# Graph attention over 128 feature rows: a product on another engine, row maxima placed by transfers, one table written later

## The chip, the core and the metric

The kernel runs on one core of a Trainium2 chip. The metric is the device time of one execution in microseconds (us); the time of a kernel is the median of several executions. The engines are TensorE (PE; its weight loads are shown apart as PEld), VectorE (DVE), ScalarE (ACT), GpSimd (POOL) and SyncE (SP), which here only issues transfers.

## The reference

The inputs are node features x (3327 x 128), a weighted adjacency matrix adj (3327 x 3327, mostly zero) and five weight matrices. Two layers follow one another, both with a residual:

```python
h = relu(layernorm(x))
x = x + relu((D^-1/2 (adj + I) D^-1/2 h) @ W0)          # layer 0
h = relu(layernorm(x))
q, k, v = ((h @ W.T).reshape(128, 3327, 8) for W in (Wq, Wk, Wv))
a = einsum('dnh,dmh->dnm', q, k) * 128**-0.5 + adj + adj  # 128 x 3327 x 3327
a = softmax(a, axis=2)
x = x + einsum('dnm,dmh->dnh', a, v).reshape(3327, 1024) @ Wo.T   # layer 1
```

Layer 1 is 128 independent attentions ("heads" below, index d), each of 3327 queries and 3327 keys with a depth of only 8, and adj is added twice to every score.

## The kernel before, in words

Layer 0 and the tables for layer 1 take the first tenth of the time. `find_edges` lists the nonzero entries of every row of adj (at most 135, 27, 20, 15 or 13 slots a row, by tile of 128 rows). Since nearly all of adj is zero, the attention is computed without adj, and the edges are added apart.

**Tables by node.** `by_nodes` (L461) turns k, v and q from one row per head into one row per node, by transposes on TensorE, copies on ScalarE (L489) and VectorE (L490) and a store: `kn_d`, `vn_d`, `qn_d`, in this order, 26 tiles of 128 nodes each.

**Edges ahead.** `over_edges` (L495) then treats the last three tiles of queries, tile by tile: for each slot a gather of 128 rows of `kn_d`, a product with q (L520), a sum over the 8 depths (L521), the bias (L525); then the maximum (L532), the exponential, a gather of `vn_d`, a product (L548) and sums on TensorE (L556). A planner of the framework orders this part. The other 23 tiles' edges go on GpSimd beside the attention (`edges_beside`): its instructions are a list with estimated times, from which `edges_on` takes some at each key tile, so that they last for a little over five sixths of the heads.

**Attention.** Queries are cut into seven chunks, in the order 383, 384, then five of 512. For every chunk there are 128 heads, so 896 heads in all; with 26 key tiles each. This part is written in its final order by hand. While head g gets its weights and output, the row maxima of heads g+1 and g+2 are computed beside it:

- `weight(t)`, for key tile t: a matmul gives 128 keys x 512 queries (`pt`, L865), ScalarE takes the exponential (`e`, L873). The operands are held in two halves of 64 partitions, and matmuls of the two halves stand beside one another.
- `products`: e times v, summed in PSUM (`po`, L892), six tiles later.
- `part` and `left`: matmuls (`ps`, L791) give scores by query, and VectorE takes their maxima (`top`, L776 and L810). `left` treats the two odd key tiles at the end of a row group. When a row is done, L818 writes `neg`, the negated maximum per query.
- `halve` (L822): GpSimd splits `neg` into two float32r numbers, `halves` (128 x 4 x 2).
- `place` (L827): four transposes (three in narrow chunks) bring the halves into two rows, `pt_max`; one tile later `below_q` copies them to two rows below q (L838, ScalarE) and from there to the second half of partitions (L839, GpSimd). The key operand has ones in these rows, so `pt` comes out less its row maximum.
- At the end of a head `evacuate` copies `po`, `fold_up` transposes it (`pt_out`), `divide` adds the four groups (L943) and the edges' part (L945, GpSimd), and `by_sums` takes the reciprocal (L954) and the product with it (`o`, L955), both on VectorE, and stores `o` to DRAM from SP (L960).

The later steps are put off by a counter of key tiles: `later(n, step)` runs a step n tiles on. `evacuate` runs in the next head at tile 5, `fold_up` five later, `divide` one later, `by_sums` eight later, at about tile 20. `attend_beside` puts the maxima's steps on tiles: the last row group of head g+1 on tiles 0 to 5 of head g, `halve` at tile 7, and `place` at

```python
behind.setdefault(t + 3, []).append(of_next[1])
behind.setdefault(min(t + 3 + PLACED, MJ - 2), []).append(of_next[2])
```

which, with PLACED = 8, is tile 15. The loads of a head's q, k, v and edges (`load`, L726) are issued by SP three heads ahead, at the start of head g for head g+3, into four buffers in turn: up to three transfers for the edges (L739), eight for q (L751), four for k (L753) and two for v (L754). SP issues in program order and waits where a transfer must wait.

Of the kernel before, what the change touches and what calls it, by code (L numbers as in the profile page):

```python
# [2 lines left out]

# [6 lines left out]
F32 = mybir.dt.float32  # L10
F32R = mybir.dt.float32r
# [22 lines left out]
U = 4  # L34
LATE = 6
FOLDED = 5
PLACED = 8
GATHERED = 27


# [43 lines left out]
def kernel(  # L84
# [376 lines left out]
    def by_nodes():  # L461

        nc.scalar.activation(factor, edge_adj, AF.Exp, scale=-2.0)
        nc.vector.tensor_scalar(factor, factor, -1.0, 1.0, ALU.mult, ALU.add)
        nc.vector.tensor_scalar(bias, edge_adj, 0.0, NO_EDGE, ALU.is_le, ALU.mult)
        nc.vector.tensor_tensor(bias, bias, edge_adj, ALU.add)
        with (
            tc.tile_pool(name="by_head", bufs=2) as by_head,
            tc.tile_pool(name="by_node", bufs=6) as by_node,
            tc.tile_pool(name="ps_turn", bufs=4, space=PSUM) as ps_turn,  # L470
        ):
            for src, dst, more in ((k_d, kn_d, 0), (v_d, vn_d, P), (q_d, qn_d, 0)):
                for n0 in range(0, N, W):
                    w = min(W, N - n0)
                    xs = by_head.tile([P, w * H], F32, tag=f"xs{w}", name="xs")
                    nc.sync.dma_start(out=xs, in_=src[:D, n0 * H : (n0 + w) * H])
                    xs = xs.rearrange("d (n h) -> d h n", h=H)
                    for i in range((w + P - 1) // P):
                        r = min(P, w - i * P)
                        ps = ps_turn.tile([P, H, P], F32, tag="ps", name="ps_turn")  # L480
                        for h in range(H):
                            nc.tensor.transpose(
                                ps[:r, h, :], xs[:, h, i * P : i * P + r], ident
                            )
                        row = by_node.tile([P, E + more], F32, tag=f"row{more}", name="row")
                        if more:
                            nc.gpsimd.memset(row[:, E:], 1.0)
                        to = row[:r, :E].rearrange("p (h d) -> p h d", h=H)
                        nc.scalar.copy(to[:, : H // 2], ps[:r, : H // 2])  # L489
                        nc.vector.tensor_copy(to[:, H // 2 :], ps[:r, H // 2 :])  # L490
                        nc.scalar.dma_start(
                            out=dst[n0 + i * P : n0 + i * P + r, :], in_=row[:r]
                        )

    def over_edges(tiles):  # L495

        with (
            tc.tile_pool(name="ps_sum", bufs=2, space=PSUM) as ps_sum,
            tc.tile_pool(name="gathered", bufs=1) as gathered,
            tc.tile_pool(name="edge", bufs=2) as edge,  # L500
        ):
# [5 lines left out]
            turn = 0  # L507
            for t in tiles:
# [172 lines left out]
    def attention(sparse):  # L681
# [3 lines left out]
        with (  # L685
# [24 lines left out]
            nc.vector.memset(halves.bitcast(F32), 0.0)  # L710
            for b in range(4):
                nc.vector.memset(qs[b].bitcast(F32), 0.0)

# [49 lines left out]
            def maxima(b, w):  # L763
# [56 lines left out]
                        )  # L820

                def halve():  # L822
                    upper, lower = halves[:, :, 0], halves[:, :, 1]
                    nc.gpsimd.tensor_copy(upper, neg)  # L824
                    nc.gpsimd.tensor_tensor(lower, neg, upper.bitcast(F32), ALU.subtract)

                def place():  # L827
                    ps = ps_s.tile([P, UNIT * P], F32, tag="ps", name="pt_max")
                    for i, r in subs:
                        nc.tensor.transpose(  # L830
                            ps[:2, i * P : i * P + r],
                            halves.bitcast(F32)[:r, i, :],
                            ident[:r, :r],
                        )

                    def below_q():
                        first, second = q_to[2 * C : 2 * C + 2, :w], q_to[64 + 2 * C : 66 + 2 * C, :w]
                        nc.scalar.copy(first, ps[:2, :w])  # L838
                        nc.gpsimd.tensor_copy(second, first.bitcast(F32))  # L839
# [10 lines left out]
            def attend(d, b, n0, w, behind, beside):  # L850
# [86 lines left out]
                def divide(pt):  # L937
# [11 lines left out]
                    def by_sums():  # L949
                        inv = small.tile([P, 4, 1], F32, tag="inv", name="inv")  # L950
                        o = small.tile([P, 4, H], F32, tag="o", name="o")
                        for i, r in of_all:
                            n = i.stop - i.start
                            nc.vector.reciprocal(inv[:r, i], both[:r, i, H : H + 1])  # L954
                            nc.vector.tensor_tensor(  # L955
                                o[:r, i], both[:r, i, :H], inv[:r, i].to_broadcast([r, n, H]),
                                ALU.mult,
                            )
                            lo = n0 + i.start * P
                            nc.sync.dma_start(  # L960
                                out=o_d[bass.ds(d, 1), lo : lo + (n - 1) * P + r, :].rearrange(
                                    "o (i p) h -> p (o i) h", i=n
                                ),
                                in_=o[:r, i],
                            )

                    later(8 if sparse else 0, by_sums)

# [200 lines left out]
```

## Time and profile before

| | us |
|---|---|
| median of 3 runs | 18434.68 (18426.49 to 18447.8) |
| profiled execution, its own time | 18442.5 |
| span of its trace, first to last instruction | 18440.7 |
| busy PE / DVE / ACT / POOL in the span | 16464.3 / 16036.7 / 13220.6 / 8699.1 |
| first and last weight matmul of the attention | 1887.2 to 18324.4 |

All times below come from this one execution. A busy engine is one with an instruction running; matmuls are pipelined and their ends are modelled, so a busy TensorE is not one at its peak. An engine's idle time is put down to the one that released it last. The chain of waits is followed back from the last instruction: at each step to what released it or to the instruction before it on its engine, so a share of the chain is time that something else would have to fill if it went. Names are those of the program, with buffer numbers left out: `o<-both,inv` is an instruction that reads both and inv and writes o. L955 is line 955 of the kernel before.

### The profile page before, as it was taken

The page shows a single profiled execution, that of the slowest core. Times are in us where ns is not written, and L with a number is a line of the kernel's source. Part 1 is how long each engine was busy: PE and PEld are TensorE (multiplying, and loading weights), DVE is VectorE, ACT ScalarE, POOL GpSimd, SP SyncE. Part 2 cuts the span into 40 slices and gives each one's busy share as a digit, 9 for nine tenths or more (in the row PEclk, how much of TensorE's full clock was granted, in tenths as well). Part 3 has the DMA queues.
Part 4 walks back from the last instruction along what each step waited for, and adds up shares of the span by engine and source line. Part 5 has one row for each costly group of instructions (what it writes and reads, how often), then busy time and mean ns, then how long its engine had stood idle before and what let it go on. Part 6 is the DMA issues. An engine that isn't in the chain of part 4 may idle for free.

```text
span 18440.7 us, 318852 instructions
## 1 busy us (share of the span) xinstructions
PE 16464.3 (89%) x106289; PEld 7120.9 (39%) x106289; DVE 16036.7 (87%) x32069; ACT 13220.6 (72%) x27107; POOL 8699.1 (47%) x13162
## 2 busy tenths in 40 slices
PE   0453888889999999999999999999999999999999
PEld 0242344444444433333333333333333333444444
DVE  9444888888888899999999999999999999999997
ACT  4221666667777777777777777777777777888886
POOL 0012665666666655555555555656565565311110
PEclk9976999999999999999999999999999999999999
DMA  2474222222222222222222222222111111111112
GB/s 82 168 254 182 59 50 50 52 49 61 58 55 60 54 52 51 52 53 54 46 54 51 56 51 54 57 59 46 41 40 39 38 40 38 41 41 40 41 40 64
DMA packets 1645778, 1139.83 MB, mean 62 GB/s; under 512 B 1383825, under 2 KB 1448588, under 8 KB 1634309
## 3 DMA queue, kind: packets, MB, share of 16 engines
q1 hardware_dynamic: 1463008, 838.80, 19.4%
q0 software_dynamic: 154656, 172.45, 3.5%
q10 hardware_dynamic: 26468, 108.06, 1.5%
q8 instruction: 857, 14.04, 0.3%
q14 instruction: 789, 6.46, 0.1%
HBM read 1372.14 MB, written 173.77 MB: 84 GB/s over the span
## 4 chain that ended last, share of the span: by engine, by line
PE 73%; DVE 13%; ACT 3%; issue 2%; DMA 2%; POOL 0%; ACTq 0%; DVEq 0%; POOLq 0%; SPq 0%
PE po L892 28%; PE pt L865 27%; PE ps L791 13%; DVE top L776 7%; DVE o L955 4%; PE pt_out L908 3%; PE pt_max L830 2%; ACT e L873 2%; ACT q L838 1%; DVE mostsb L1060 1%; DVE inv L954 0%; DMA vn_d<-row 0%; DMA kn_d<-row 0%; DMA qn_d<-row 0%; PE po_last L1128 0%
## 5 line engine op out<-in xcount | busy, mean ns | idle before, releaser
L873 ACT ACTIVATE e<-pt 128x512 f32<-128x512 f32 (+3 forms) x23296 | 11843.5, 571 | 3720.2 <-PE ps L791 2248.8
L776 DVE TENSOR_REDUCE top<-ps 128x1 f32<-128x512 f32 x19968 | 12574.8, 682 | 1445.0 <-PE ps L791 1254.4
L865 PE MATMUL pt<-q,k 64*128 64x512 f32 (+2 forms) x23296 | 8553.2, 445 | 93.0 <-ACT e L873 51.4
L791 PE MATMUL ps<-k,q 64*128 64x512 f32 (+1 forms) x26624 | 7628.4, 400 | 671.0 <-DVE top L776 626.0
L892 PE MATMUL po<-e,v 128*32 128x512 f32 (+3 forms) x46592 | 6419.7, 585 | 22.2 <-issue 3.4
L865 PEld LDWEIGHTS pt<-q,k 64*128 64x128 f32 (+1 forms) x23296 | 3751.6, 188 | 6677.3 <-ACT e L873 6277.6
L791 PEld LDWEIGHTS ps<-k,q 64*128 64x128 f32 x26624 | 4193.7, 188 | 1010.1 <-DVE top L776 795.5
L824 POOL CAST halves<-neg 128x4 fp32r<-128x4 f32 x896 | 167.5, 187 | 4113.0 <-PE pt L865 1921.6
L892 PEld LDWEIGHTS po<-e,v 128*32 128x32 f32 (+1 forms) x46592 | 1008.7, 108 | 1542.1 <-issue 1227.3
L810 DVE TENSOR_REDUCE top<-ps 128x1 f32<-128x128 f32 (+2 forms) x3584 | 1262.5, 392 | 0.0
L839 POOL CAST q<-q 2x512 fp32r<-2x512 f32 (+2 forms) x896 | 514.8, 575 | 1516.2 <-ACT q L838 747.0
L1060 POOL TENSOR_TENSOR productb<-vgb,scoresb 128x1152 f32<-128x1152 f32 x452 | 1195.9, 2646 | 13.2
L1060 POOL TENSOR_TENSOR sumsb<-sumsb,productb 128x1152 f32<-128x1152 f32 x452 | 1195.4, 2645 | 11.9
L1060 POOL TENSOR_TENSOR productb<-kgb,qnb 128x1024 f32<-128x1024 f32 x475 | 1125.4, 2369 | 12.9
L1060 POOL TENSOR_TENSOR productb<-productb 128x512 f32<-128x512 f32 (+1 forms) x950 | 951.5, 1002 | 43.4
L955 DVE TENSOR_TENSOR o<-both,inv 128x32 f32<-128x32 f32 (+3 forms) x1152 | 816.6, 709 | 39.4
L945 POOL TENSOR_TENSOR both<-both,hope 128x36 f32<-128x36 f32 (+3 forms) x1152 | 258.5, 233 | 1169.7 <-DVE both L943 1161.9
L292 PE MATMUL tr_unfit<-ident,peak 128*1 128x128 f32 x1 | 0.4, 373 | 667.6 <-DVE peak L291 667.6
L449 POOL DMA_INDIRECT kgb<-kn_d,edge_col x475 | 522.6, 1100 | 133.7 <-issue 109.5
L449 POOL DMA_INDIRECT vgb<-vn_d,edge_col x475 | 517.2, 1089 | 120.2 <-issue 74.6
L908 PE MATMUL pt_out<-ident,ot 128*128 128x128 f32 (+1 forms) x3328 | 562.4, 289 | 10.5 <-DVE top L776 9.6
L838 ACT CAST q<-pt_max 2x512 fp32r<-2x512 f32 (+2 forms) x896 | 487.0, 544 | 93.0 <-PE pt_max L830 71.5
(163 smaller groups left out, 8209.2 us busy)
## 6 DMA issues: line engine op xcount, KB each, us to landing
k<-kt_d SPq DMA_DIRECT2D x3584, 104.0 KB
nat<-v_d SPq DMA_DIRECT2D x1792, 52.0 KB
a<-in_adj_dram SPq DMA_DIRECT2D x25, 1663.5 KB
q<-qt_d SPq DMA_DIRECT2D x1280, 32.0 KB
q<-qt_d SPq DMA_DIRECT2D x2560, 16.0 KB
at<-in_adj_t_dram SPq DMA_DIRECT2D x30, 1280.0 KB
qt_d<-heads_t ACTq DMA_DIRECT2D x16, 1664.0 KB
kt_d<-heads_t ACTq DMA_DIRECT2D x16, 1664.0 KB
```

The lines of the kernel that those rows point to most:

```text
L449: nc.gpsimd.indirect_dma_start(to, None, table[:, :], bass.IndirectOffsetOnAxis(edge_col[:, slot : slot + 1].bitcast(U32), 0), bounds_chec ...
L776: nc.vector.tensor_reduce(to, ps, AX.X, ALU.max)
L791: nc.tensor.matmul(ps, q_to[rows, i * P : (i + 1) * P], k_by[rows, j0 * P : j1 * P], start=True, stop=True,)
L810: nc.vector.tensor_reduce(top[:, rows[0] : rows[-1] + 1, 6 + c], parts[:, : len(rows)], AX.X, ALU.max,)
L838: nc.scalar.copy(first, ps[:2, :w])
L839: nc.gpsimd.tensor_copy(second, first.bitcast(F32))
L865: nc.tensor.matmul(ps[:m, :even], ks[b % 4][rows, j * P : j * P + m], qs[b % 4][rows, :even], start=True, stop=True,)
L873: nc.scalar.activation(e[:m, :w], ps[:m, :w], AF.Exp, scale=2.0)
L892: nc.tensor.matmul(po[0][g * R : (g + 1) * R, :w], vb[:m, t % 2, t // 2, :], es.pop(t)[:m, :w], start=(t < 4), stop=(t + 4 >= MJ),)
L908: nc.tensor.transpose(ps[:r, i * P : (i + 1) * P], ot[:, i * P : i * P + r], ident)
L955: nc.vector.tensor_tensor(o[:r, i], both[:r, i, :H], inv[:r, i].to_broadcast([r, n, H]), ALU.mult,)
L1060: step()
```

## The change

Three parts.

1. **The product.** In `by_sums` the product `o` goes from VectorE to GpSimd. The store is a step of its own, six tiles later, so in the next head's first tile.
2. **The maxima.** `halve` writes two buffers in turn, laid out as 128 x 2 x 4. `place` is three transfers on SP: `halves` to a small DRAM tensor `most_d` (2 x 512, four in turn), and from there the two rows to each half of q. The transposes, `below_q` and its two copies go. PLACED is 1, so `place` is at tile 8. The first transfer has 128 x 8 pieces of one float each, since neighbouring queries lie on neighbouring partitions.
3. **q's table.** `by_nodes` writes only k's and v's tables. `over_edges` opens the same pools (two PSUM buffers for the transposes in place of four) and writes q's table itself: first the six tiles of nodes that the three tiles of queries need, then the other 20, four after every seventh slot. It first computes the scores of all three tiles, each in a buffer of its own, and then goes on to the maxima and the sums of all three, with one PSUM buffer for the sums in place of two.

```diff
-PLACED = 8
+PLACED = 1
...
+    most_d = [dram.tile([2, W], F32, name=f"most{b}_d") for b in range(4)]
...
-            for src, dst, more in ((k_d, kn_d, 0), (v_d, vn_d, P), (q_d, qn_d, 0)):
-                for n0 in range(0, N, W):
...
+        with relayout_pools(4) as turn:
+            for src, dst, more in ((k_d, kn_d, 0), (v_d, vn_d, P)):
+                for n0 in range(0, N, W):
+                    turn(src, dst, more, n0)
...
         with (
-            tc.tile_pool(name="ps_sum", bufs=2, space=PSUM) as ps_sum,
+            relayout_pools(2) as turn_q,
+            tc.tile_pool(name="ps_sum", bufs=1, space=PSUM) as ps_sum,
...
+            q_from = sorted(range(0, N, W), reverse=True)
+            while q_from and q_from[0] + W > min(tiles) * P:
+                turn_q(q_d, qn_d, 0, q_from.pop(0))
...
-                scores = edge.tile([P, GATHERED, D], F32, tag="scores", name="scores")
+                scores = gathered.tile([P, slots, D], F32, name=f"scores{t}")
+                scores_of[t] = scores
...
+                    if turn % 7 == 0 and q_from:
+                        turn_q(q_d, qn_d, 0, q_from.pop(0))
+            for n0 in q_from:
+                turn_q(q_d, qn_d, 0, n0)
+            for t in tiles:
+                (to, r), slots, s0 = edges_of(t), SLOTS[t], FIRST_SLOT[t]
+                scores = scores_of[t]
...
-            halves = fixed.tile([P, 4, 2], F32R, name="halves")
+            halves = [fixed.tile([P, 2, 4], F32R, name=f"halves{b}") for b in range(2)]
...
                 def place():
-                    ps = ps_s.tile([P, UNIT * P], F32, tag="ps", name="pt_max")
-                    for i, r in subs:
-                        nc.tensor.transpose(
-                            ps[:2, i * P : i * P + r],
-                            halves.bitcast(F32)[:r, i, :],
-                            ident[:r, :r],
+                    nc.sync.dma_start(
+                        out=most_d[b % 4].rearrange("x (i p) -> p (x i)", p=P),
+                        in_=halves[b % 2].bitcast(F32).rearrange("p x i -> p (x i)"),
+                    )
+                    for c in range(2):
+                        lo = 64 * c + 2 * C
+                        nc.sync.dma_start(
+                            out=q_to.bitcast(F32)[lo : lo + 2, :w], in_=most_d[b % 4][:, :w]
                         )
-
-                    def below_q():
-                        first, second = q_to[2 * C : 2 * C + 2, :w], q_to[64 + 2 * C : 66 + 2 * C, :w]
-                        nc.scalar.copy(first, ps[:2, :w])
-                        nc.gpsimd.tensor_copy(second, first.bitcast(F32))
-
-                    later(1, below_q)
...
-                            nc.vector.tensor_tensor(
+                            nc.gpsimd.tensor_tensor(
                                 o[:r, i], both[:r, i, :H], inv[:r, i].to_broadcast([r, n, H]),
                                 ALU.mult,
                             )
...
+                        later(6 if sparse else 0, store)
```

More of the change, by code (lines that the diff above doesn't have):

```diff
@@ L469, in by_nodes @@
             tc.tile_pool(name="by_node", bufs=6) as by_node,
-            tc.tile_pool(name="ps_turn", bufs=4, space=PSUM) as ps_turn,
+            tc.tile_pool(name="ps_turn", bufs=bufs, space=PSUM) as ps_turn,
         ):
-            for src, dst, more in ((k_d, kn_d, 0), (v_d, vn_d, P), (q_d, qn_d, 0)):
-                for n0 in range(0, N, W):
[L474 to L481, printed above, removed]
-                            nc.tensor.transpose(
[L483 to L493, printed above, removed]
@@ new lines, in turn @@
+            def turn(src, dst, more, n0):
+                w = min(W, N - n0)
+                xs = by_head.tile([P, w * H], F32, tag=f"xs{w}", name="xs")
+                nc.sync.dma_start(out=xs, in_=src[:D, n0 * H : (n0 + w) * H])
+                xs = xs.rearrange("d (n h) -> d h n", h=H)
+                for i in range((w + P - 1) // P):
+                    r = min(P, w - i * P)
+                    ps = ps_turn.tile([P, H, P], F32, tag="ps", name="ps_turn")
+                    for h in range(H):
+                        nc.tensor.transpose(ps[:r, h, :], xs[:, h, i * P : i * P + r], ident)
+                    row = by_node.tile([P, E + more], F32, tag=f"row{more}", name="row")
+                    if more:
+                        nc.gpsimd.memset(row[:, E:], 1.0)
+                    to = row[:r, :E].rearrange("p (h d) -> p h d", h=H)
+                    nc.scalar.copy(to[:, : H // 2], ps[:r, : H // 2])
+                    nc.vector.tensor_copy(to[:, H // 2 :], ps[:r, H // 2 :])
+                    nc.scalar.dma_start(
+                        out=dst[n0 + i * P : n0 + i * P + r, :], in_=row[:r]
+                    )
@@ L708, in attention @@
             negs = [fixed.tile([P, 4], F32, name=f"neg{b}") for b in range(4)]
-            halves = fixed.tile([P, 4, 2], F32R, name="halves")
-            nc.vector.memset(halves.bitcast(F32), 0.0)
+            halves = [fixed.tile([P, 2, 4], F32R, name=f"halves{b}") for b in range(2)]
+            for b in range(2):
+                nc.vector.memset(halves[b].bitcast(F32), 0.0)
             for b in range(4):
@@ L822, in halve @@
                 def halve():
-                    upper, lower = halves[:, :, 0], halves[:, :, 1]
+                    upper, lower = halves[b % 2][:, 0], halves[b % 2][:, 1]
                     nc.gpsimd.tensor_copy(upper, neg)
@@ L958, in by_sums, with store @@
                             )
[L959 to L965, printed above, removed]
+                        def store():
+                            for i, r in of_all:
+                                n = i.stop - i.start
+                                lo = n0 + i.start * P
+                                nc.sync.dma_start(
+                                    out=o_d[
+                                        bass.ds(d, 1), lo : lo + (n - 1) * P + r, :
+                                    ].rearrange("o (i p) h -> p (o i) h", i=n),
+                                    in_=o[:r, i],
+                                )
+                        later(6 if sparse else 0, store)
                     later(8 if sparse else 0, by_sums)
```

8 lines of the change are left out of this document (6 added, 2 removed).

## The prediction

> **What bounds the kernel now.** I read the chain of waits first, then cut the attention, 89% of the span (1887 to 18330 us), into its four stages by windows, and read the chain, the groups and the timeline of each.
>
> ```profile
> PE 73%; DVE 13%; ACT 3%; issue 2%; DMA 2%; POOL 0%; ACTq 0%; DVEq 0%; POOLq 0%; SPq 0%
> ```
>
> Columns of the next view: start:end, length, busy time of each engine with its instructions, granted TensorE clock, DMA share, GB/s.
>
> ```profile
> core 0: us, PE busy (x) PEld busy (x) DVE busy (x) ACT busy (x) POOL busy (x), PEclk, DMA share, GB/s
> 1900.00:4140.00 2240.00, 1994.78 (x13658) 913.75 (x13656) 1879.44 (x4073) 1555.26 (x3943) 1411.42 (x2578) 0.93 0.23 51
> 4140.00:6240.00 2100.00, 1977.87 (x14045) 878.87 (x14045) 1783.78 (x3435) 1568.29 (x3791) 1343.67 (x1877) 0.98 0.25 58
> 6250.00:15750.00 9500.00, 9137.92 (x58539) 3748.65 (x58536) 8838.21 (x15972) 7442.52 (x14472) 5378.81 (x7246) 0.98 0.22 49
> 15850.00:18250.00 2400.00, 2395.14 (x15675) 987.95 (x15675) 2241.08 (x4251) 1970.71 (x3852) 294.99 (x1071) 1.00 0.19 41
> ```
>
> The rows are heads of 383 queries (128 of them, 17.5 us each), of 384 (128, 16.4 us), of 512 with edge work on GpSimd (499 in this window, 19.04 us) and of 512 without (2400 / 18.07 us = 133). In the last, TensorE is busy 99.8% of the time and is the bound. In the others it idles 4 to 11% while VectorE is 84 to 93% busy. The chain of each window, in that order, says what ends last there:
>
> ```profile
> by line: PE pt L865 21.4%; PE po L892 21.1%; DVE top L776 13.6%; DVE o L955 9.6%; PE ps L791 8.8%; ACT e L873 7.7%; issue 4.8%; PE pt_out L908 2.5%; ACT q L838 2.3%; PE pt_max L830 2.1%; DVE inv L954 1.8%; DVE mostsb L1060 0.8%; DMA kgb<-kn
> by line: PE pt L865 24.6%; PE po L892 22.7%; DVE top L776 17.9%; PE ps L791 9.1%; ACT e L873 9.0%; DVE o L955 3.8%; issue 3.1%; PE pt_out L908 2.9%; ACT q L838 2.8%; PE pt_max L830 2.5%; DVE mostsb L1060 0.7%; DVE inv L954 0.5%; ACT scoresb
> by line: PE po L892 33.1%; PE pt L865 31.6%; PE ps L791 16.6%; DVE top L776 5.6%; DVE o L955 4.5%; PE pt_out L908 3.0%; PE pt_max L830 2.7%; issue 0.7%; DVE mostsb L1060 0.7%; ACT e L873 0.4%; DVE inv L954 0.3%; ACT scoresb L604 0.2%; DVE m
> by line: PE po L892 38.8%; PE pt L865 36.3%; PE ps L791 18.3%; PE pt_out L908 3.3%; PE pt_max L830 2.9%; issue 0.2%; DVE top L776 0.1%; DVE o L955 0.0%; DVE inv L954 0.0%
> ```
>
> The line that moves to GpSimd (`DVE o L955`) holds 9.6%, 3.8%, 4.5% and 0.0%; the four transposes (`PE pt_max L830`) hold 2 to 3% everywhere. Why L955 matters only beside edge work (count, then shortest/median/longest ns):
>
> ```profile
> L955 DVE TENSOR_TENSOR o<-both,inv x496: 191/994/3092, 6255.7 to 15736.4; 128x32 f32<-128x32 f32 x166
> L955 DVE TENSOR_TENSOR o<-both,inv x132: 191/191/607, 15867.2 to 18234.0; 128x32 f32<-128x32 f32 x132
> ```
>
> Without GpSimd work it takes 191 ns; with it the median is 994 and the longest 3092, longer than GpSimd's longest edge instruction (mean 2646 ns). TensorE pays at the small "left" matmuls that follow it (idle time before them at the end; three windows in order):
>
> ```profile
> L791 PE MATMUL ps<-k,q 64*128 64x128 f32 x762 | 161.2, 280 | 202.3 <-DVE top L776 201.7
> L791 PE MATMUL ps<-k,q 64*128 64x128 f32 x785 | 150.4, 273 | 82.9 <-DVE top L776 82.9
> L791 PE MATMUL ps<-k,q 64*128 64x128 f32 x3968 | 594.2, 263 | 305.7 <-DVE top L776 303.9
> ```
>
> **Product to GpSimd.** DVE loses L955; a 128x32 product on GpSimd is nearest to L945 (252 ns at 512 queries, 233 over all), and GpSimd loses L839's copy (605 and 575), so it gets about 350 ns lighter per head.
>
> ```profile
> L839 POOL CAST q<-q 2x512 fp32r<-2x512 f32 (+2 forms) x896 | 514.8, 575 | 1516.2 <-ACT q L838 747.0
> L945 POOL TENSOR_TENSOR both<-both,hope 128x36 f32<-128x36 f32 (+3 forms) x1152 | 258.5, 233 | 1169.7 <-DVE both L943 1161.9
> ```
>
> What returns is at most L955's share of the chain, at least the left matmuls' idle less what the edge reductions (`mostsb`, 0.7 to 0.8%) still cause.
> 383: idle 202 less 18 = 184. 384: 83 less 15 = 68. 512 with edges: idle 306 less 67 = 239 at the low end; at the high end, against heads without edge work, 499 x (19.04 - 18.07) less 67 = 417, near L955's own 4.5% (428). I take 370: VectorE, left with 8838 - 475 = 8363 us over 499 heads, 16.8 us each, then runs at 95% of the new head, so a few waits stay. Last stage: 0. Sum 622, bounds 491 and 669. GpSimd now waits at that product for the reciprocal; queued behind it are edge instructions and the next halves, but GpSimd already idles 3440 us before the halves, so it has the time.
>
> The Trainium skill (SBUF — State Buffer, Who interferes with whom) says that a VectorE instruction with one SBUF input does not contend with GpSimd. By that the reciprocal and the reductions left on VectorE would wait for nothing and the sum would be the upper bound; the mean of 167 ns for the reciprocal agrees.
>
> **Transposes and copies gone.** TensorE loses `pt_max`: 2.1% of 2240 = 47, 2.5% of 2100 = 53, 2.7% of 9500 = 257, 2.9% of 2400 = 70, sum 427 us (0.5 us a head). ScalarE loses L838 (574 ns, on the chain at 2.3% and 2.8% of the narrow heads, 110 us); ScalarE is 70 to 82% busy, so I count none of it and keep it for the range.
>
> **Three transfers in their place.** This is free only while they land before the next head's first weight matmul. The first writes 1024 pieces of 4 bytes to DRAM; the other two, two rows each, wait for it on SP. They start at the halves (tile 7) and are due at tile 0:
>
> ```profile
> 17013.70 0.20 POOL L825 TENSOR_TENSOR halves<-neg,halves 128x4 fp32r<-128x4 f32 x1
> ...
> 17024.87 0.49 PE L865 MATMUL pt<-q,k 64*127 64x512 f32 x1
> ...
> 17026.28 0.50 PE L865 MATMUL pt<-q,k 64*128 64x512 f32 x1
> ```
>
> From the end of the halves (17013.90) to tile 0 there are 12.4 us, 11.8 once the transposes in between (0.60) are gone. In heads of 384 queries the halves stand 8.4 to 10.4 us before tile 25; with the 1.4 us to tile 0 and 0.4 taken off, 9.4 at least. The price: a store of 512 pieces of 32 bytes, and a load that waits for it,
>
> ```profile
> 18330.17 0.37 SPq L960 DMA_DIRECT2D o_d<-o  x1
> 18334.10 1.32 SPq L1117 DMA_DIRECT2D o_rows<-o_d  x3
> ```
>
> stand 3.9 us apart. The first transfer has 512 pieces more, 32 on each of 16 engines. A packet costs, on the mean,
>
> ```profile
> q1 hardware_dynamic: 1463008, 838.80, 19.4%
> ```
>
> 0.194 x 16 x 18440.7 / 1463008 = 39 ns, so 32 x 39 = 1.25 us more: 5.2. Two issues add 0.5 (a zeros load holds SP 0.23) and a landing 2.9 at most (at the start of the attention, last key load issued by 1847.51, first matmul 1850.45). Together 8.6 us, under 11.8 and just under 9.4: hidden, 0 us. Upper end for a small write: all DMA time of a head without edges (0.19 x 16 x 18.07 = 55 us) charged to its 512 store pieces, 107 ns; then the first transfer is 3.9 - 1.25 + 64 x 0.107 = 9.5 and the chain 12.9. Behind the wait on SP stand the next head's loads. They cannot use their buffers before the next head starts, and SP now spends 8822 us, 9.8 per head, waiting for L955, a wait that goes; the store, moved six tiles later behind the next loads, finds its product done. The second buffer of `halves` costs nothing: its reader of two heads ago is done. I price SP at nothing; without that cover 5 us a head would be late for loads that have a whole head of time.
>
> The skill's page DMA: Bandwidth & Descriptors (rules for kernel authors) speaks against this: a last dimension that isn't contiguous becomes one descriptor per element, and under 512 bytes the engine reads before it writes. Its fixed cost is about 2.0 us per transfer, so two rounds in turn would be an estimated 4 us plus the pieces: hidden as well.
>
> **q's table between the edges.** Before, q's share of the relayout takes 1510 to 1587 us and the first edge product stands at 1619. Only 6 of its 26 tiles now stand ahead: start 20/26 x 77 = 59 us earlier. The score stage is 39 x (1.21 + 1.87) = 120 us of VectorE plus 20 copies at 0.69 = 14. The sums of all three tiles then follow at TensorE's pace (1.94 us a slot when VectorE only feeds it, 1790 to 1809): 39 x 1.94 = 76, plus 5 for the first maxima. So 1619 - 59 + 215 = 1775, against 1813: 38 us, bounds 0 (the copies wait for their loads) and 59.
>
> Sum: 622 + 427 + 38 = 1087, less about 5 for the first head's transfers, which nothing hides: 1082. The profiled run took 18442.5 us (span 18440.7, 2 around it), 8 over the median of 18434.7; from the median, 18434.7 - 1082 = 17,353. I say 17,350.
>
> **The rivals.** (1) The transfers are late: slower. The 4-byte writes go to lines that neighbouring pieces share; nothing in the trace shows such a store. Being x late at 512 queries (640 heads) means x + 2.4 at the 256 narrow ones; 640x + 256(x + 2.4) = 1082 gives x = 0.5, a chain of 12.3 us, 97 ns a piece. At 107 ns, x = 1.1: 704 + 896 - 1082 = 518 slower, 18,950, and rising 0.9 ms for each further us. For it: 4 bytes is the smallest piece in the kernel. Against: 39 ns is a mean over packets of 570 bytes, and 512 stores of 32 bytes a head fit in it. (2) Half hidden: late only in the narrow heads, by up to 2 us (512 us back), or VectorE's waits stay because other reductions take over: 427 + 38 and little else. 17,600 to 17,970. (3) The product waits on GpSimd behind 2.6 us edge instructions and delays the halves: GpSimd is 57% busy at 512 queries; 1 us a head in the edge stages, 0.75 ms, would leave about 18,100.
>
> **How the numbers follow.** Forecast 0.60, its own range 17,150 to 17,650 (upper bounds of the parts: 669 + 427 + 110 + 59). Rivals (2) and (3) together 0.17, rival (1) 0.20, a sum within 0.2% of before (37 us, about what a measurement of this kernel can tell) 0.03. Range 17,130 to 18,200: all but the late transfers.
>
> **What would show it.** Right: no `pt_max` and no L955 in the chain, TensorE at 98% or more in all stages, heads of 512 near 17.5 without and 17.8 with edges. Wrong: TensorE's weight matmul at tile 0 waiting for DMA `q<-most_d`, SP's queue waiting longest there, or `top L776` still ahead of idle left matmuls.

## The result, and the profile after

| | us |
|---|---|
| before, median of the runs beside it | 18439.56 (18426.49 to 18447.8) |
| after, median of 4 runs | 19138.73 (19130.1 to 19146.46) |
| ratio | 1.038 (95% interval 1.0362 to 1.0398) |
| forecast | 17350 (17130 to 18200) |
| profiled execution after: own time, span | 19144.93, 19143.1 |

The changed kernel is slower by 699 us, outside the range; rival (1), the late transfers, came true. The lines of the kernel after: weight matmul L885 (before L865), left matmuls L816 (L791), product `o` L975 (L955), first transfer L853, the two loads L859, store of `o` L984.

The chain of waits after, by engine and by line:

```profile
PE 52%; DMA 31%; DVE 5%; issue 2%; SPq 1%; ACT 1%; POOL 1%; another core or an unknown queue 0%; POOLq 0%; ACTq 0%; DVEq 0%
PE pt L885 20%; PE po L912 20%; DMA most_d<-halves 19%; DMA q<-most_d 10%; PE ps L816 10%; DVE top L801 3%; PE pt_out L928 2%; ACT e L893 1%; DVE top L835 1%; DMA vn_d<-row 1%; DVE mostsb L1086 0%; SPq L859 0%; PE sums L580 0%; DVE neg L843 0%; POOL halves L850 0%
```

The old product and the transposes are gone from it, as forecast, and VectorE fell from 13% to 5%. But DMA rose from 2% to 31%, and 29 of these points are two names: the store `most_d<-halves` and the load `q<-most_d`. The waits of TensorE and of SP's queue name the same pair (total us, times, longest):

```profile
PE pt L885 <- DMA q<-most_d: 1246.5, 761, 13.2
...
SPq L859 <- DMA most_d<-halves: 8504.9, 882, 13.1
```

Stretches of time inside the four stages (383, 384, 512 with edges, 512 without; columns as in the prediction's second view):

```profile
2000.00:4400.00 2400.00, 1920.92 (x12424) 901.18 (x12423) 1563.82 (x3461) 1386.27 (x3573) 1309.43 (x2638) 0.85 0.27 46
4800.00:6800.00 2000.00, 1668.17 (x10857) 765.82 (x10854) 1339.37 (x2610) 1194.21 (x2912) 1043.44 (x1504) 0.86 0.29 49
7500.00:16500.00 9000.00, 8557.21 (x53864) 3532.32 (x53860) 8003.32 (x14738) 6740.33 (x13313) 4947.38 (x6902) 0.98 0.28 49
17500.00:18800.00 1300.00, 1270.20 (x8146) 528.69 (x8145) 1196.17 (x2214) 1011.70 (x2000) 122.85 (x572) 1.00 0.23 41
```

In the narrow stages TensorE is busy only 80 and 83% of the time, and the granted clock is 0.85 and 0.86, where before it was 0.93 and 0.98. One head of the last stage, from the timeline (start, length):

```profile
17001.19 0.20 POOL L850 TENSOR_TENSOR halves<-neg,halves 128x4 fp32r<-128x4 f32 x1
...
17002.63 0.45 SPq L853 DMA_DIRECT2D most_d<-halves  x1
17012.39 0.58 SPq L859 DMA_DIRECT2D q<-most_d  x2
...
17015.17 0.46 PE L885 MATMUL pt<-q,k 64*128 64x512 f32 x1 [1.52 <-DMA q<-most_d]
```

SP issues the store at 17002.63 and can issue the load only at 17012.39, 9.8 us later, when the store has landed. The load takes 2.8 us to the matmul. The prediction gave 5.2 to the first of these and 2.9 to the second. The median from store to load over some 300 us of each stage is 10.6, 10.1, 10.4 and 10.0 us.

Yet the packets of this queue look no busier:

```profile
q1 hardware_dynamic: 2402016, 849.36, 21.4%
```

That is 939,008 packets more than before (1463008), but 0.214 x 16 x 19143.1 = 65,546 us of packet time against 57,240 before, some 9 ns for each new one. By this row the store would be harmless: the time lies in the wait for the writes to finish, which it does not hold. The row of the queue that GpSimd's own transfers use, mostly the gathers of edges, does show it. Before, after, and in two experiments below (e_nowait, with the same store, and e_apart, with its pieces 64 bytes apart):

```profile
q0 software_dynamic: 154656, 172.45, 3.5%
q0 software_dynamic: 154656, 172.45, 5.9%
q0 software_dynamic: 154656, 172.45, 6.4%
q0 software_dynamic: 154656, 172.45, 3.7%
```

The same packets took 10,327 us before and 18,071 after (0.059 x 16 x 19143.1), and 10,286 in e_apart: the store slows transfers that have nothing to do with it.

The mean time of a head in each stage, from ScalarE's one copy of `po` per head, puts all runs beside one another (us):

| kernel | 383 | 384 | 512, edges | 512, none | time, median |
|---|---|---|---|---|---|
| before | 17.71 | 16.17 | 19.15 | 18.06 | 18439.56 |
| after | 20.28 | 19.33 | 19.07 | 18.23 | 19138.73 |
| e_product | 15.61 | 15.59 | 18.28 | 18.06 | 17659.91 |
| e_old_place | 15.63 | 15.61 | 18.27 | 18.06 | 17633.71 |
| e_nowait | 18.40 | 17.58 | 18.33 | 17.86 | 18267.93 |
| e_apart | 15.27 | 15.31 | 17.99 | 17.77 | 17371.72 |
| e_dense | 18.09 | 16.23 | 18.36 | 17.79 | 18059.94 |
| e_columns | 15.73 | 15.35 | 17.98 | 17.76 | 17443.84 |

### The profile page after: what moved, and what is told of

Its sections match the earlier page's. It is cut to its first block, busy times and chain, and to the rows that moved or that the text cites. A ratio compares the mean times of both kernels' runs of the same rounds, so it can differ in the third digit from the quotient of the medians.

```text
span 19143.1 us, 311703 instructions
## 1 busy us (share of the span) xinstructions
PE 16464.4 (86%) x102961; PEld 7215.5 (38%) x102961; DVE 15277.9 (80%) x30918; ACT 12619.1 (66%) x26212; POOL 8390.7 (44%) x13418
## 3 DMA queue, kind: packets, MB, share of 16 engines
q1 hardware_dynamic: 2402016, 849.36, 21.4%
## 4 chain that ended last, share of the span: by engine, by line
PE 52%; DMA 31%; DVE 5%; issue 2%; SPq 1%; ACT 1%; POOL 1%; another core or an unknown queue 0%; POOLq 0%; ACTq 0%; DVEq 0%
PE pt L885 20%; PE po L912 20%; DMA most_d<-halves 19%; DMA q<-most_d 10%; PE ps L816 10%; DVE top L801 3%; PE pt_out L928 2%; ACT e L893 1%; DVE top L835 1%; DMA vn_d<-row 1%; DVE mostsb L1086 0%; SPq L859 0%; PE sums L580 0%; DVE neg L843 0%; POOL halves L850 0%
## 5 line engine op out<-in xcount | busy, mean ns | idle before, releaser
L885 PE MATMUL pt<-q,k 64*128 64x512 f32 (+2 forms) x23296 | 8478.6, 448 | 1394.9 <-DMA q<-most_d 1246.5
L816 PE MATMUL ps<-k,q 64*128 64x512 f32 (+1 forms) x26624 | 6988.0, 400 | 81.7 <-DVE top L801 57.5
L885 PEld LDWEIGHTS pt<-q,k 64*128 64x128 f32 (+1 forms) x23296 | 3859.5, 193 | 8368.9 <-ACT e L893 6569.2
L912 PE MATMUL po<-e,v 128*32 128x512 f32 (+3 forms) x46592 | 6613.3, 599 | 22.1 <-issue 3.4
L816 PEld LDWEIGHTS ps<-k,q 64*128 64x128 f32 x26624 | 4150.1, 195 | 311.4 <-DVE top L801 114.1
L975 POOL TENSOR_TENSOR o<-both,inv 128x32 f32<-128x32 f32 (+3 forms) x1152 | 247.9, 225 | 1976.8 <-DVE inv L974 1392.2
L946 POOL TENSOR_TENSOR hope<-hope,by 128x36 f32<-128x36 f32 (+3 forms) x1152 | 255.3, 231 | 748.1 <-ACT by L945 747.2
```

The lines of the kernel that those rows point to most:

```text
L816: nc.tensor.matmul(ps, q_to[rows, i * P : (i + 1) * P], k_by[rows, j0 * P : j1 * P], start=True, stop=True,)
L885: nc.tensor.matmul(ps[:m, :even], ks[b % 4][rows, j * P : j * P + m], qs[b % 4][rows, :even], start=True, stop=True,)
L912: nc.tensor.matmul(po[0][g * R : (g + 1) * R, :w], vb[:m, t % 2, t // 2, :], es.pop(t)[:m, :w], start=(t < 4), stop=(t + 4 >= MJ),)
L946: nc.gpsimd.tensor_tensor(hope[:r, i, 1:], hope[:r, i, 1:], by[:r, i].rearrange("p (i o) -> p i o", o=1).to_broadcast([r, i.stop - i.start ...
L975: nc.gpsimd.tensor_tensor(o[:r, i], both[:r, i, :H], inv[:r, i].to_broadcast([r, n, H]), ALU.mult,)
```

## The experiments

**e_store: what does the first transfer cost by itself?** A small kernel issues, three times each, a store in some pattern and then a load of two rows that depends on it.

```diff
+    case("rowh", 8, 1024, rows(8))       # as in the kernel: 1024 floats side by side
+    case("rowa", 1, 1024, rows(1))       # 128 floats in one 512-byte row
+    case("apart", 8, 1024 * 16, apart)   # 1024 floats, 64 bytes apart
+    case("own", 8, 2048, own)            # a partition's eight floats in 64 bytes of its own
+    case("inload", 8, 1024, whole, back=lambda d: d.rearrange("(p x i) -> x i p", x=2, i=4))
...
```

> This kernel leaves the reference's computation out: it measures stores alone, on an otherwise idle core. Each case is a store from 128 partitions to DRAM, then a load of 2 rows that waits for it, three times in turn; the gap from one issue to the next on SP's queue is the price. In the changed kernel the store of 1024 pieces of 4 bytes stood 9.5 to 10.8 us before the load that waits for it; the forecast had 5.2. Theory A, a price per piece: the gap grows in a line with the pieces, so with 9.6 us at 1024 and some 2.6 fixed, 512 pieces take 6.1, 256 take 4.4 and 128 take 3.5; where the pieces lie (64 bytes apart, or two floats apart by partition) and their size (8, 16, 32 bytes) change nothing, so 512 pieces of 32 bytes take 6 as well, and the 3.9 that the forecast took for it is beaten. Theory B, shared lines: neighbouring pieces of 4 bytes fall into one line of DRAM from different queues; with pieces 64 bytes apart the gap falls to the forecast's 5.2 and pieces of 32 bytes stay at 3.9. Theory C, the rest of the kernel's transfers: alone, 1024 pieces take the forecast's 5.2. 128 contiguous pieces of 32 bytes take about 3 by all of them. The load of 1024 scattered floats into two partitions and the eight direct transfers from partitions to a row are there for their price alone: by A the first is far over 10 us, the second 8 issues at 0.3 and 3 us of landing.

Timeline lines of the third round of three cases (`rowh` as in the kernel, `apart`, `own`):

```profile
58.49 0.36 SPq L42 DMA_DIRECT2D dst_rowh<-src_rowh  x1
67.84 0.24 SPq L44 DMA_DIRECT2D land<-dst_rowh  x1
...
189.41 0.36 SPq L42 DMA_DIRECT2D dst_apart<-src_apart  x1
192.28 0.24 SPq L44 DMA_DIRECT2D land<-dst_apart  x1
...
209.71 0.52 SPq L42 DMA_DIRECT2D dst_own<-src_own  x1
216.24 0.22 SPq L44 DMA_DIRECT2D land<-dst_own  x1
```

| store | store's issue to load's issue, us |
|---|---|
| 1024 floats side by side (the kernel's) | 9.3, 9.35 (first round 12.9) |
| 512, 256 floats side by side | 8.7 to 9.0; 8.3 to 8.95 |
| 128 floats side by side | 7.5 to 8.3 |
| 1024 floats 64 bytes apart | 2.5 to 2.9 |
| 1024 floats 8 bytes apart, the eight of a partition in 64 bytes of its own (`own`) | 6.0 to 6.7 |
| 1024 floats side by side, issued by ScalarE; by GpSimd | 9.7 to 11.4; 9.0 to 9.1 |
| 1024 pieces of 8, of 16 bytes, side by side | 4.6 to 4.9; 2.9 to 3.3 |
| 512 pieces of 32 bytes (like `o`) | 1.8 to 2.6 |
| 128 pieces of 32 bytes, one after another | 1.4 to 1.5 |

An eighth of the pieces takes nearly as long, so there is no price per piece. The same pieces apart take 2.5 to 2.9, so there is no price for being 4 bytes either. And the 9.3 us appear with none of the kernel's traffic around. What is left is nearness: pieces that lie close to one another in DRAM hold one another up. They need not come from different partitions: in `own` each partition writes into 64 bytes of its own, and the store still takes 6.0 to 6.7. Nor is it the queue, since the store is as slow when ScalarE or GpSimd issues it. The load behind also lands later: 3.5 us from its issue to the copy behind a slow store, 1.3 to 1.5 behind `apart`. Gathering on the way back (`inload`) has its own price: store 1.4, load 5.6 to 7.2.

**e_lines: how near is too near?** The same 1024 floats at 4, 8, 16, 32, 64 and 128 bytes from one another, and a way without DRAM: eight transfers, each of one column of 128 floats into a row of q, then one copy of two rows inside SBUF.

```diff
+    for name, o in (("near", 1), ("two", 2), ("four", 4), ("eight", 8), ("sixteen", 16), ("more", 32)):
+        case(name, 8, 1024 * o, apart(o))
+    case("one", 1, 128 * 16, apart(16))
+    chain("chain", 4)
+    chain("short", 3)
```

> Leaves the reference's computation out; stores alone again, on an idle core. 1024 pieces of 4 bytes in the order of the changed kernel, 4, 8, 16, 32, 64 and 128 bytes apart, then 128 pieces 64 bytes apart. Theory B says that pieces within one line wait for one another, so the gap falls with every doubling until the spacing is a line, and stays at 2.5 to 2.9 us from there: the spacing at which it stops falling is the line. In e_store 8-byte pieces side by side took 4.7 us and 16-byte ones 3.0, so a line should be 32 or 64 bytes. 128 pieces 64 bytes apart: about 2 us, against 7.5 to 8.3 side by side. Theory A (a price per piece) is out already and would have all of them at 9.3. Then the chain of a way without DRAM, for its price: one transfer for each column of halves straight into q's row (eight, or six in narrow heads), then one that copies the two rows to the other half: eight columns took 5.2 us in e_store, the copy adds some 2, so 7.2, and 6.5 for six.

| bytes apart | 4 | 8 | 16 | 32 | 64 | 128 |
|---|---|---|---|---|---|---|
| store's issue to load's issue, us | 9.3 | 4.5 to 4.9 | 3.0 to 3.5 | 2.7 to 2.8 | 2.4 to 2.6 | 2.6 to 3.0 |

The 9.3 at 4 bytes is e_store's; here transfers of `short` came in between (9.3, 11.7, 13.9). Over a floor of 2.5 the excess is on the mean 6.8, 2.2, 0.8 and 0.2: it shrinks with each doubling, and from 32 bytes on it is no larger than the scatter at 128, so these runs do not tell whether a stretch of 32 or of 64 bytes counts. The 8- and 16-byte pieces of e_store, side by side, take as long as 4-byte pieces 8 and 16 bytes apart, so for this order of pieces the distance decides and not the size (`own`, at 8 bytes but with a partition's pieces together, takes longer than the 4.5 to 4.9 here). 128 floats 64 bytes apart took 1.4 to 2.3, against 7.5 to 8.3 side by side. The eight columns and the copy took 8.4 to 9.3 us from the first issue to the landing, where 7.2 was expected. The six of `short` gave no clean number: they got mixed with the slow stores, and once SP issued the fourth of them only 10.5 us after the third.

**e_nowait: is it only the wait?** The kernel after, with the loads reading zeros: the stores remain, nothing waits for them, and the row maxima are left out of the exponentials.

```diff
-                            out=q_to.bitcast(F32)[lo : lo + 2, :w], in_=most_d[b % 4][:, :w]
+                            out=q_to.bitcast(F32)[lo : lo + 2, :w], in_=zeros_d[:, :w]
```

> The changed kernel, but the two loads into q's rows read the tensor of zeros and so wait for nothing; the store of 1024 pieces and its traffic stay. It leaves the row maxima out of the exponentials. Theory A, the chain of transfers is the whole loss and the rest is worth what the forecast said: 17,350 (17,150 to 17,650), TensorE waits for nothing at the head's first weight matmul, heads of 512 queries at 17.5 without edges and 17.8 with. Theory B, the store's traffic itself slows the other transfers, or the other parts are worth less: above 17,800. Theory C, the wait on SP is not what TensorE waits for: 19,140 stays.

18267.93 us (18257.37 to 18269.35), ratio 0.991 (0.9894 to 0.9927): far from 17,350. TensorE's waits, and a stretch of the 383 stage:

```profile
PE pt L885 <- DMA q<-zeros_d: 417.6, 169, 10.9
```

```profile
2000.00:3800.00 1800.00, 1530.25 (x10284) 711.92 (x10281) 1290.37 (x2863) 1139.76 (x2954) 1081.82 (x2176) 0.91 0.35 51
```

This is theory B: SP issues these loads 0.48 us after the store in the median and never more than 2.3 us, yet TensorE waits for them, up to 10.9 us. They go through the same DMA queue as the slow store and come in behind it; that GpSimd's queue slows down too (q0 above, 6.4%) says that order in one queue is not all of it. So the store does harm in two ways: by the wait (871 us, from 19,138.73), and by standing in the way.

**e_apart: the same pieces, other addresses.** e_nowait with the pieces 64 bytes apart in DRAM.

```diff
-    most_d = [dram.tile([2, W], F32, name=f"most{b}_d") for b in range(4)]
+    most_d = [dram.tile([2 * W, 16], F32, name=f"most{b}_d") for b in range(4)]
...
-                        out=most_d[b % 4].rearrange("x (i p) -> p (x i)", p=P),
+                        out=most_d[b % 4].rearrange("(y p) o -> p y o", p=P)[:, :, 0],
```

> As e_nowait (the loads read zeros, the row maxima are left out of the exponentials), but the 1024 pieces of the store go 64 bytes apart in DRAM; their number, size, queues and issue are the same. In e_nowait TensorE still waited for the loads of zeros, 9% of the chain, since they stand behind the store's pieces in the same queues. Theory B, pieces of one line of DRAM from different queues wait for one another: alone the store fell from 9.3 to 2.7 us with this spacing, so the loads land in time, and the time is that of e_old_place less its transposes, 17,634 - 427 = 17,207 (17,150 to 17,300). Theory A, each piece has its price wherever it goes: e_nowait's 18,268 stays.

17371.72 us (17367.56 to 17376.24), ratio 0.9422 (0.9406 to 0.9437). The chain by engine:

```profile
PE 81%; DVE 6%; ACT 2%; DMA 1%; issue 1%; POOL 1%; SPq 0%; ACTq 0%; POOLq 0%; DVEq 0%
```

DMA is at 1%, and the same number of packets (2402016) in the same queue costs 896 us less than in e_nowait. Only addresses differ between the two. The time is 72 us above the range that was stated for it (17,150 to 17,300): that range took the transposes at 427 us, and they are worth 262 (below).

**e_product and e_old_place: the other parts.** e_product is the kernel before with the product on GpSimd and the store six tiles later, nothing else. e_old_place is the kernel after with the transposes and copies back at tile 15.

```diff
 e_product, against before
-                            nc.vector.tensor_tensor(
+                            nc.gpsimd.tensor_tensor(
...
+                        later(6 if sparse else 0, store)
 e_old_place, against after
-PLACED = 1
+PLACED = 8
...
-                    nc.sync.dma_start(
-                        out=most_d[b % 4].rearrange("x (i p) -> p (x i)", p=P),
+                    ps = ps_s.tile([P, UNIT * P], F32, tag="ps", name="pt_max")
+                    for i, r in subs:
+                        nc.tensor.transpose(
...
```

> The kernel before with the first part alone: the product on GpSimd, its store six tiles later. The forecast's step: 622 us less (491 to 669), so 17,815 (17,765 to 17,945). Rival, VectorE's other instructions are late in its place, or GpSimd's wait for the reciprocal delays the halves: less than 300 us gained, above 18,130.

> The changed kernel with the transposes and copies of before in place of the transfers, at tile 15: parts one and three alone. Against the run with the product alone it shows q's table: the trace of after has the first row maxima ready 30 us earlier than before, so 30 us less than that run (forecast: 38). Against the changed kernel: some 1,300 us less if the transfers are the loss. By the forecast's steps 17,785; by the rival of the run with the product alone, above 18,100.

e_product: 17659.91 us (17656.94 to 17669.77), ratio 0.9581 (0.9565 to 0.9597), 778 us less than before. e_old_place: 17633.71 (17632.11 to 17640.05), ratio 0.9566 (0.955 to 0.9582), 26 us less again, which is q's table. Both stand below what was stated for them (17,765 to 17,945, and 17,785), because the product gains more than the forecast's step. In the groups of e_product the product is short and waits off the path:

```profile
L955 POOL TENSOR_TENSOR o<-both,inv 128x32 f32<-128x32 f32 (+3 forms) x1152 | 247.6, 224 | 606.6 <-DVE inv L954 461.1 <-issue 126.7 <-POOL q L839 13.1
```

224 ns on GpSimd against 709 on VectorE. e_old_place and the kernel after differ in the transfers in place of the transposes and copies, and they stand 1,505 us apart.

**e_dense: the store whole, the loads gathering.** `halves` goes to DRAM as it lies (32 bytes a partition), and four loads of one row each pick floats 32 bytes apart.

```diff
-                        out=most_d[b % 4].rearrange("x (i p) -> p (x i)", p=P),
+                        out=most_d[b % 4],
...
+                                in_=most_d[b % 4][:, 4 * x : 4 * x + n_rows].rearrange(
+                                    "p (o i) -> o i p", o=1
+                                ),
```

> The whole change with another way through DRAM: the store is contiguous, 32 bytes a partition (1.4 us alone), and four loads of one row each gather floats 32 bytes apart, so the small pieces are read and no line is written twice. Nothing is left out. Theory B: the store stands 1.5 to 2.5 us before the loads, these land in 3 to 6 us, the chain of 5 to 9 us is under the 9.4 to 11.8 that there are, TensorE does not wait at the first weight matmul, and the time is 17,634 - 427 = 17,207, up to 17,350 where narrow heads wait a little. Rival: small pieces are slow on the reading side too (2048 of them a head, over few queues), the chain stays over 10 us, and the time is above 18,000.

18059.94 us (18055.06 to 18088.11), ratio 0.9801 (0.9784 to 0.9817): better than before, worse than the transposes, as its rival had it (above 18,000). One head's store and loads:

```profile
12000.89 0.33 SPq L853 DMA_DIRECT2D most_d<-halves  x1
...
12002.53 5.99 SPq L860 DMA_DIRECT2D q<-most_d  x4
```

The loads now stand 1.6 us behind the store, and the four loads hold SP for 5.99 us in issuing alone. TensorE waits 465.7 us for `q<-most_d`. The price went from the scattering to the gathering.

**e_columns: no DRAM at all.** The kernel after, with one transfer for each column of `halves` straight into its row of q, and one copy of the two rows to the other half.

```diff
+                    for x in range(2):
+                        for i in range(n_rows):
+                            nc.sync.dma_start(
+                                out=q_rows[lo + x : lo + x + 1, i * P : (i + 1) * P],
+                                in_=halves[b % 2].bitcast(F32)[:, x, i : i + 1],
+                            )
                     nc.sync.dma_start(
+                        out=q_rows[64 + lo : 66 + lo, : n_rows * P],
+                        in_=q_rows[lo : lo + 2, : n_rows * P],
                     )
```

> The 4-byte pieces and the lines of DRAM that they share are left out altogether: every column of the row maxima (one tile's 128 numbers) goes by its own transfer from 128 partitions of halves straight into the row of q where it belongs (eight transfers at 512 queries, six in the narrow heads), and one copy of these two rows inside SBUF fills the other half of q's partitions. Nothing is left out of the computation; no transposes, no copies on ScalarE and GpSimd, no store to DRAM. Alone on the chip eight such transfers and the copy took 8.4, 8.4 and 9.3 us from the first issue to the landing; the deadline of the heads of 512 queries is 11.8 us, and six columns, by three quarters of the issues (5.05 us for eight), take some 7 us where 9.4 are to be had. Theory (only pieces that share lines are late; small pieces as such are not): hidden, and the time is that of the kernel with its pieces apart, 17,372, within 17,300 to 17,450, TensorE waiting for no transfer. Rival (any chain of several transfers in turn is stretched by the head's own traffic in the same queues, as the gathering loads were): beside the loads and stores of the head the chain is 3 us or more longer than alone; at 512 queries it is then 0.5 to 3 us late, 300 to 1,900 us over 640 heads, and the time is 17,700 or more, above the version that keeps the transposes (17,634), with TensorE waiting for q.

17443.84 us (17438.32 to 17454.52), ratio 0.9468 (0.9452 to 0.9484), within its range. Of the kernels that bring the maxima to q it is the fastest, 190 us under e_old_place. One head, and the waits of TensorE and SP:

```profile
12011.86 0.19 POOL L849 TENSOR_TENSOR halves<-neg,halves 128x4 fp32r<-128x4 f32 x1
12012.21 5.26 SPq L855 DMA_DIRECT2D q<-halves  x8
...
12019.01 0.66 SPq L859 DMA_DIRECT2D q<-q  x1
```

```profile
PE pt L886 <- DMA q<-q: 45.8, 44, 2.9
...
SPq L859 <- DMA q<-halves: 1410.0, 1287, 4.5
```

It has as many small pieces as the kernel after (2425056 packets), and they too land side by side, but in SBUF. It has two transfers in turn as there, and four to six more issues on SP. But the copy starts 6.8 us after the first issue, not 9.8, and TensorE waits 45.8 us in all where it waited 1246.5. At 512 queries the heads equal those of e_apart; most of the 72 us between the two are in the 383 stage (15.73 against 15.27, 128 x 0.46 = 59).

## Why the prediction was wrong, step by step

**The step that failed: the price of the first transfer.** The text took the store and load of `o` (3.9 us) and added 512 pieces at 39 ns, 1.25 us. Measured is 9.8 to 10.6 us for the store alone, so the chain is 10.2 + 2.6 = 12.8 at 512 queries with edges (medians of the whole stage) against the deadline of 11.8. The transfers were taken as hidden, 0 us; against e_apart, where none of them is late, they cost 19138.73 - 17371.72 = 1,767 us (1,505 against e_old_place, which pays for the transposes in their place). The nearest row was the right one to start from: e_store repeats it (512 pieces of 32 bytes, 1.8 to 2.6). The wrong part was the addition. The mean time of a packet says what the queue spends on it, not when a write close beside others is done. The text had the mechanism in rival (1), "lines that neighbouring pieces share", and set it aside by that mean; what the runs show of it is nearness in DRAM (e_lines, e_apart), not how the writes hold one another up.

**Rival (1)** said a chain of 12.9 us and 18,950. The chain fits and the time is 189 us off, but its price was right by accident: 107 ns a piece is not a price per piece, since 128 pieces take 7.5 to 8.3 us. Against e_apart its two terms are, by heads of the table, 704 forecast and some 610 measured at 512 queries (1.08 and 0.46 a head), 896 forecast and 1,156 measured in the narrow heads (5.01 and 4.02 x 128). The narrow ones lose more than they wait: TensorE's median wait at tile 0 there is 3.6 and 2.8 us. The same stretches show the clock at 0.85 and 0.86 where e_apart has 1.00 and 0.99, so the rest goes along with the clock. The Trainium skill (TensorE: Matmul & The Clock Gate, Part 1) says that some 3.4 us without work bring the clock down. The stages agree in kind: with median waits of 0.6 us, at 512 queries with edges, it stayed at 0.98, as it was before. No run changed the clock alone.

**The DMA page's rule.** By the skill's fixed cost (DMA: Bandwidth & Descriptors, Anatomy of one DMA: a fit to transfers on GpSimd's path, where these are SP's) the text had an estimate of 4 us plus the pieces. In e_store a store of 32 bytes a partition (1.4 to 1.5) and the load of two rows behind it (1.4 to 1.6) stay under it; the kernel's own pair took 12.8. The page's warning that a last dimension that is not contiguous becomes one descriptor per element (rules for kernel authors) held, with 1,048 packets more per head; the estimate from its fixed cost did not reach the case.

**Product to GpSimd: right, too small.** 622 forecast, bounds 491 and 669, measured 778, above the upper bound. By stage, in heads: 383, 184 forecast and 2.10 x 128 = 269 measured; 384, 68 and 74; 512 with edges, 370 and 0.87 x 507 = 441; without edges 0 and 0. The 383 heads gained more than TensorE's idle time before the left matmuls, and their clock rose from 0.93 to 1.00; no run takes the two apart. In the 512 heads with edges the forecast put 499 heads of 19.04 us into its window. There were 496, as the row of L955 that it shows says, of 19.15 us. The head that its 370 us lead to, (9500 - 370) / 499 = 18.30, is the one measured, 18.28; the head before was read 0.11 us too short, 0.11 x 507 = 56 of the 71 us that are missing. Rival (3), edge instructions ahead of the product, did not come: GpSimd waits 461.1 us for the reciprocal, and nobody on the path waits for that.

**Transposes gone: right, too large.** 427 forecast, and 17633.71 - 17371.72 = 262 measured, with the copies included. The chain's share (0.52 us a head) was taken as removable. Two slots of the kernel before, from weight matmul to weight matmul, show that it was not; the first holds the transposes, the second the same other matmuls without them:

```profile
17018.17 0.50 PE L865 MATMUL pt<-q,k 64*128 64x512 f32 x1
...
17018.83 0.60 PE L830 MATMUL pt_max<-ident,halves 128*2 128x128 f32 x4
...
17021.03 0.49 PE L865 MATMUL pt<-q,k 64*128 64x512 f32 x1
...
17023.68 0.50 PE L865 MATMUL pt<-q,k 64*128 64x512 f32 x1
```

2.86 us with and 2.65 without: 0.21 a head, 188 us over 896 heads. Measured at 512 queries without edges is 0.29 (18.06 to 17.77). So this could be read before the run: a slot without the work was there to compare with.

**q's table: right,** 26 measured, 38 forecast, bounds 0 and 59. SP was priced at nothing, and rightly: it now waits 8504.9 us for the store, in place of 8821.6 for the product, and TensorE waited for a load of k twice, 16.4 us in all, and for the loads of q's own rows not at all.

The errors of the three gains nearly cancel, by luck (156 too little, 165 and 12 too much): e_apart, with all of them and no transfer late, stands at 17,371.72 against the 17,350 of the forecast. Of the 1,789 us that the forecast missed, 1,767 are the transfers. What stays open is the law of the excess: it falls faster than the number of pieces in 64 bytes, a partition's own pieces hold one another up as well, and no run here tells whether near writes queue in the memory or in the DMA engines.

## What to carry to other kernels

Before a transpose goes to DMA, look at how close its pieces lie to one another in DRAM: 4-byte pieces side by side took some 6 to 7 us longer than the same pieces 64 bytes apart, with 128 of them as with 1024, and the packet row of their own queue did not show it. Such a store also held back what was queued behind it and the gathers of another queue. And where the transfers came late TensorE's granted clock was lower too (0.85 and 0.86), so a miss of 2.8 to 3.6 us cost 4.0 to 5.0. A transfer from SBUF straight into the row, one for each column, took 190 us off the version with transposes. And cost a group that goes by comparing a slot that has it with one that has not.

## What the runs showed of the hardware

- 128 floats written side by side from 128 partitions took 7.5 to 8.3 us, and 1024 took 9.3; 64 bytes apart they took 1.4 to 2.3 and 2.4 to 2.9.
- Eight floats of one partition, 8 bytes apart in 64 bytes of its own, were slow as well: 6.0 to 6.7 us for 1024 (e_store, `own`).
- TensorE waited up to 10.9 us for a load that waits for nothing, behind such a store in its queue (e_nowait), and two rows took 3.5 us to land behind the kernel's store alone, 1.3 to 1.6 behind the patterns that are not side by side floats (e_store).
- The packets of GpSimd's queue took 1.75 times as long beside such stores (18,071 us against 10,327) and as long as before beside the same pieces 64 bytes apart (10,286).
- Four loads that gather single floats into one row each hold SP for 5.99 us of issuing; eight transfers of a column into a row, 5.26 us.
